# A graph attention kernel: the row carried between superchunks as row 0 of the sums, and 112 nodes per superchunk

## The chip, the cores and the metric

One core of one Trainium2 chip. The time is that of one execution on the device, in microseconds (us). The engines are TensorE (PE, its weight loads PEld), VectorE (DVE), ScalarE (ACT), GpSimd (POOL) and SyncE (SP), each with an instruction stream of its own; they wait for each other through semaphores. In profile lines "L1245" is line 1245 of the kernel file.

## What is computed

Two layers of graph attention over 6250 nodes and 200000 edges (each edge has a source, a destination and 32 attributes; the edges come sorted by destination). Cut to what matters:

```python
def _gat(x, src, dst, ea, Wg, a_s, a_d, Wge, a_e, b, n, h, f):
    hx = (x @ Wg).reshape(n, h, f)
    he = (ea @ Wge).reshape(-1, h, f)
    al = leaky_relu((hx*a_s).sum(-1)[src] + (hx*a_d).sum(-1)[dst] + (he*a_e).sum(-1), 0.2)
    m = segment_max(al, dst)
    al = exp(al - m[dst])
    al = al / segment_sum(al, dst)[dst]
    return segment_sum(hx[src] * al[:, :, None], dst).reshape(n, h * f) + b

def _forward(x, ...):                       # h = 4 heads in layer 0, 1 head in layer 1
    te = relu(edge_attr @ We0 + be0) * exp(x @ Wo0 + bo0)[src][:, None]
    x = relu(_gat(x, *_add_self_loops(src, dst, te, n), ...) + x)     # layer 0
    te = relu(edge_attr @ We1 + be1) * exp(x @ Wo1 + bo1)[src][:, None]
    return _gat(x, *_add_self_loops(src, dst, te, n), ...) + x + orig  # layer 1

h = maximum(layernorm(x), 0)
result = x + _forward(h, ...)
```

## The kernel before

**Tiling.** The sorted edges are cut into 1563 chunks of 128 (one edge per partition), and the chunks into 66 superchunks per layer: 64 of 24 chunks, then one of 14 and one of 13. One superchunk of one layer is a step; there are 132 steps, k = 0 to 131, layer 0 first. A superchunk covers the nodes from its first destination (its base) on; no superchunk of this graph spans more than 102 nodes. Since the edges are sorted, the last node of a superchunk can go on in the next one, so part of its sums must be carried over.

**One step.** For a superchunk, `gather` (POOL, L928) fetches the table row of each edge's source: 24 indirect DMAs of 128 rows into the tile G, with a memset of an unused tile, `gap` (L932), after each. There are three G buffers, and the gathers run two steps ahead: those of step k+2 may start when the sums of step k-1 have read their buffer. `rphase1` makes the edge terms (PE y L1014, ACT R L1019, PE zad L1028), `logits` (DVE, L1115 and on) the attention logits, `links` and `maxima` the running maxima over a node's edges: a PE transpose into lf (L1138), two scans on DVE (L1148, L1150), a transpose back (L1155), then the softmax weights. `scale` (DVE, L1223) multiplies G by the weights, 6.5 us. `onehots` (DVE, L1058) builds S: for each edge of each chunk a one-hot row of 128 columns, by comparing `k_iota` (0 to 127, kept in PSUM) with the edge's destination less the base. `sums` (PE, L1234) adds S^T G over the chunks into u (PSUM, one buffer): row n of u is the sum over the edges of node base + n. `evict` (ACT, L1239) copies u to U.

**The carried row.** `carry` (L1245, L1247) picks the row of the superchunk's last node: PE multiplies `lsel`, a one-hot column with its 1 at the last node's place, with U, and ACT copies the resulting single row to `carry`. In the next step `carried` (DVE, L1208 to L1213) adds that row, times a weight `pr`, to row 0 of the next G before the next `sums`.

**Nodes.** `nodes` loads the 128 table rows from the base on (tw) and, in layer 0, the rows of x. `finish` (merge and nodes, from L1258 on) adds the self loop, divides, and applies the activation, on 128 partitions for a node each. `rows1` to `rows3` make the rows of layer 1's table from it (PE transpose L1329, ACT h1T L1331, PE L424, DVE L428), stored to T[1]; in layer 1 the result goes to out. Neighbouring superchunks overlap in the rows they store; the later store wins. The last two of layer 1 use an indirect store with a bounds check.

**Order.** The order on each engine is written by hand in `edges` (steps up to 60 and 66 to 126 of the main loop), `tight` (near a layer's end) and `last`. In the main loop one step issues, in this order: gathers of the next-but-one superchunk (by `gather(nx)` with its buffer), logits, the edge terms of the next step, links, rows2 of an earlier step, maxima, scale, carried, sums, rows3, onehots of the next step, finish of the previous step, evict, carry, rows1 of the previous step. So on PE, between the sums of one step and the sums of the next, stand in this order: fin of `carry` (waits for U), turned rows L1329, lf L1138, the zad of the node terms (L1073), y L1014, L1155, the table rows L424, the second y, zad, and then the sums, which wait for `carried` and for u to be evicted.

A check on the indices (`chk`) verifies what the fast path assumes, among it that no superchunk spans more nodes than a tile has; otherwise a general path runs.

Of the kernel before, what the change touches and what calls it, by code (L numbers as in the profile page):

```python
# [31 lines left out]
P = 128  # L32
C = 24
SE = P * C
NX = 24
D = 256
ED = 32
PH = 64
BIG = 1e38
PAD_DST = 1 << 20  # L40
END_DST = 1 << 22
EPS = 1e-5
# [36 lines left out]
class Kernel:  # L79
# [31 lines left out]
    def consts(self, wp):  # L111
# [33 lines left out]
                       allow_small_or_imprecise_dtypes=True)  # L145

        self.kps = k = self.ps_k.tile([P, 512], F32, name="kps")
        V.tensor_copy(k[:, 0:P], self.iota_f)
        m32 = wp.tile([P, 1], F32, name="m32", bufs=1)
        self.quad = cp.tile([P, 4], F32, name="quad")  # L150
        nc.gpsimd.memset(self.quad, 0.0)
# [5 lines left out]
        self.k_iota, self.k_part, self.k_w = k[:, 0:P], k[:, P:P + 1], k[:, 2 * P:2 * P + 4 * C + 4]  # L157
        self.wea = []
        for L in self.L:
            wea = cp.tile([P, PH], F32, name=f"wea{L.l}")  # L160
# [269 lines left out]
    def indices(self, wp):  # L430
# [29 lines left out]
        V.tensor_scalar(self.qsel.rearrange("p s k -> p k s"), qd, self.iota_p, None, op0=OP.add)  # L460
        yield

        bcf = wp.tile([NS, 4], F32, name="bcf", bufs=1)
# [32 lines left out]
        V.tensor_scalar(self.base_i[:, 1, :], base[0:1, :], float(N - P), None, op0=OP.min)  # L496
        yield
        ll = wp.tile([P, NS], F32, name="ll", bufs=1)
        V.tensor_sub(ll, last, base)
        self.lsel = cp.tile([P, NS], F32, name="lsel")  # L500
        V.tensor_scalar(self.lsel, ll, self.iota_p, None, op0=OP.is_equal)
        yield
        self.slink = cp.tile([1, NS], F32, name="slink")
        V.tensor_tensor(self.slink, sc0[0:1, 0, :], sc0[0:1, 2, :], op=OP.is_equal)
# [2 lines left out]

        chk = wp.tile([1, 9, NS + 1], F32, name="chk", bufs=1)
        V.memset(chk, 0.0)
        V.tensor_scalar(chk[:, 0, :NS], ll[0:1, :], float(P - 1), None, op0=OP.is_gt)  # L510
# [4 lines left out]
        yield  # L515
        V.memset(nb[:, NS:], float(N))
        V.tensor_sub(nb[:, :NS], nb[:, 1:], nb[:, :NS])
        V.tensor_scalar(chk[:, 1, :NS], nb[:, :NS], float(P), None, op0=OP.is_gt)
        V.tensor_scalar(chk[:, 2, :NS], nb[:, :NS], 0.0, None, op0=OP.is_lt)
        yield  # L520
        V.tensor_tensor(chk[:, 3, :NS], sc0[0:1, 0, :], sc0[0:1, 2, :], op=OP.is_lt)
        if self.direct:
            V.tensor_scalar(chk[:, 4, :self.direct], base[0:1, :self.direct], float(N - P), None, op0=OP.is_gt)
# [87 lines left out]
    def edges(self, ctx):  # L611
# [32 lines left out]
        for k, st in enumerate(steps):  # L644
            nx = steps[k + 1] if k + 1 < len(steps) else None
            for q in steps[k + 1:k + 3]:
                if q["L"] is st["L"] and "tw" not in q:
                    self.nodes(q)
            self.load_lb(k + 2)
            left = self.groups[self.ahead][0] - 2 - k if self.ahead < len(self.groups) else 99  # L650
            if self.rest is None and left <= 2:
                gi = self.index_load(self.ahead, self.xp)
                self.rest = self.index_group(self.ahead, self.xp, gi)
            if st["s"] + 1 == self.NS:
                self.last(st, pv, nx)
# [36 lines left out]
            self.edge_rows(nx)  # L692
            self.onehots(nx)
            if pv:
                drain(self.finish(pv))
            if enter:
                pr = pv
            else:
                self.evict(st)
                self.carry(st)  # L700
                if pv:
                    self.rows1(pv)
                    late = pv
# [23 lines left out]
    def tight(self, st, pv, pr, nx):  # L727
# [36 lines left out]
            self.rows3(pv)  # L764
        drain(self.maxima(st))
        if final:
            self.carry(pv)
            drain(y)
            self.load_ea(st["k"] + 2)
        else:  # L770
            self.evict(pv)
        self.rphase2(nx)
        self.adst(nx)
        if not final:
            self.carry(pv)
            if pr:
                self.rows1(pr)
                self.rows2(pr)
# [10 lines left out]
    def last(self, st, pv, nx):  # L789
# [20 lines left out]
        drain(self.maxima(st))  # L810
        if pv:
            self.evict(pv)
            self.carry(pv)
        drain(self.scale(st, 3))
        self.carried(st)
        self.sums(st)
# [167 lines left out]
    def row(self, i, s):  # L984

        return self.nc.values_load(self.base_i[0:1, i, s:s + 1], engines=(mybir.EngineType.SP,), min_val=0,
                                   max_val=self.N - i * P, skip_runtime_bounds_check_because="destinations are nodes")

    def nodes(self, st):
        nc, L, s = self.nc, st["L"], st["s"]  # L990
        r = self.row(0, s)
        tw = self.np_.tile([P, self.L[0].TW + D], F32, name="tw", bufs=5)
        st["tw"], st["xw"] = tw[:, :L.TW], tw[:, L.TW:L.TW + D]
        w = L.TW + L.l * D
        nc.sync.dma_start(tw[:, :w], self.T[L.l][ds(r, P), 0:w])
        if L.l == 0:
            nc.sync.dma_start(st["xw"], self.a["x"][ds(r, P), :])

    def halves(self, st):

# [30 lines left out]
    def spread(self, st):  # L1031


        if "Q" in st:
            return
        V = self.nc.vector
        q = self.pair(st["k"]) or [st]
        if len(q) < 2 or q[0]["C"] != q[1]["C"]:
            q = [st]
        i, n, s = len(q), 32 * st["C"], st["s"]  # L1040
        lb = st["lb2"] if i > 1 else st["lb"].unsqueeze(1)
        Q = self.wp.tile([P, 2, P], BF, name="Q")
        V.tensor_tensor(lb[:, :, :n], lb[:, :, :n], self.k_part.unsqueeze(2).to_broadcast([P, i, n]), op=OP.is_equal)  # L1043
        V.tensor_tensor(Q[:, :i].rearrange("p i (k j) -> p (i k) j", j=32),
                        self.k_iota[:, 0:32].unsqueeze(1).to_broadcast([P, 4 * i, 32]),
                        self.qsel[:, s:s + i, :].rearrange("p i k -> p (i k)").unsqueeze(2)
                        .to_broadcast([P, 4 * i, 32]), op=OP.is_equal)
# [188 lines left out]
    def evict(self, st):  # L1236
        L = st["L"]
        st["U"] = U = self.np_.tile([P, 272], F32, name="U", bufs=3)
        self.nc.scalar.activation(U[:, :L.W], st["u"][:, :L.W], AF.Copy)  # L1239

    def carry(self, st):
        nc, L, s, U = self.nc, st["L"], st["s"], st["U"]
        if s + 1 < self.NS:
            pr = self.ps_f.tile([P, 512], F32, name="fin")
            nc.tensor.matmul(pr[0:1, :L.W], self.lsel[:, s:s + 1], U[:, :L.W], start=True, stop=True)  # L1245
            st["carry"] = cv = self.wp.tile([1, 272], F32, name="carry")
            nc.scalar.activation(cv[:, :L.W], pr[0:1, :L.W], AF.Copy)  # L1247

    def merge(self, st, wp, w):

# [346 lines left out]
```

## Times and profile before

| what | value |
|---|---|
| median of three runs | 4719.46 us (4714.36 to 4720.51) |
| the profiled execution | 4718.23 us, of which the span of its records 4716.0 us |
| mean granted TensorE clock | 0.732 |
| busy: POOL, PE, DVE, ACT | 3701.8, 3214.2, 2878.5, 574.2 us |
| gathers: number, mean | 3102, 959 ns |
| gap memsets: number, mean | 3102, 221 ns |
| mean period of a steady step, layer 0 and layer 1 | 34.60 us and 34.42 us (start of U to start of U) |

A group line reads: line, engine, operation, output <- inputs, shape, count | busy time, mean ns of one | idle time of the engine just before them, and the releaser that ended most of it. A line of the waits reads: who waited, for whom, total us, times, longest. A timeline line reads: start, duration, engine, line, operation, and in brackets the idle time before it and what ended it. "remote" is a release that the profile can't put down to an instruction of this core. The ends of matmuls are modelled, so the recorded end of a group of matmuls may differ from the moment their result is there.

### The profile page before, as it was taken

What the parts mean: (1) busy time and instruction counts of PE and PEld (TensorE: products, weight loads), DVE (VectorE), ACT (ScalarE), POOL (GpSimd) and SP (SyncE); (2) the same over time, 40 slices, a digit from 0 to 9 for tenths busy, and PEclk for the clock granted to TensorE, in tenths of its full rate; (3) what the DMA queues carried; (4) which work ended last, traced back from release to release, by engine and by line L of the source; (5) the groups of instructions that cost most, each with busy time, mean ns of one, the idle gap of its engine ahead of it and who ended that gap; (6) DMA issues with size and microseconds to landing.
All of it is one profiled execution on the core that took longest, in us unless ns stands there. A gap on an engine that the chain in (4) does not pass through costs nothing.

```text
span 4716.0 us, 38255 instructions
## 1 busy us (share of the span) xinstructions
PE 3214.2 (68%) x10176; PEld 1915.8 (41%) x10176; DVE 2878.5 (61%) x6552; ACT 574.2 (12%) x1282; POOL 3701.8 (78%) x6350
## 2 busy tenths in 40 slices
PE   7777767777677776777655666666666666656666
PEld 6444444444444443444422333434333343433334
DVE  7566767667676676766743555546455555645555
ACT  5111111111111111111100001000000100000010
POOL 5688888888888888888648888888888888888884
PEclk9677777767777777777866677777767776777778
DMA  6344444444444444444323444444444444444442
GB/s 216 111 129 126 136 122 129 134 122 135 127 134 127 124 136 123 132 131 124 107 84 104 128 118 126 125 112 127 120 127 118 126 126 111 127 118 128 118 124 63
DMA packets 236364, 584.09 MB, mean 124 GB/s; under 512 B 63097, under 2 KB 91007, under 8 KB 236073
## 3 DMA queue, kind: packets, MB, share of 16 engines
q0 software_dynamic: 150144, 422.75, 33.8%
q1 hardware_dynamic: 85579, 158.16, 10.1%
q8 instruction: 82, 1.34, 0.1%
q14 instruction: 143, 1.17, 0.1%
q10 hardware_dynamic: 416, 0.67, 0.1%
HBM read 547.11 MB, written 34.33 MB: 123 GB/s over the span
## 4 chain that ended last, share of the span: by engine, by line
DVE 40%; another core or an unknown queue 33%; PE 16%; issue 6%; ACT 4%; POOL 0%; DMA 0%; SPq 0%; DVEq 0%; ACTq 0%; POOLq 0%
DVE G L1223 16%; DVE S L1058 8%; PE y L1014 8%; PE fin L1245 3%; DVE rt L1101 2%; ACT R L1019 1%; ACT U L1239 1%; DVE ade L1104 1%; PE fin L1329 1%; PE u L1234 1%; PE lf L1138 1%; PE zad L1028 1%; DVE mt L1172 1%; DVE m L1175 1%
## 5 line engine op out<-in xcount | busy, mean ns | idle before, releaser
L928 POOL DMA_INDIRECT G<-T,src x3102 | 2974.0, 959 | 938.3 <-issue 498.2
L1234 PE MATMUL u<-G,S 128*128 128x270 f32 (+1 forms) x6252 | 1469.7, 393 | 110.3 <-issue 58.0
L1234 PEld LDWEIGHTS u<-G,S 128*128 128x128 f32 x6252 | 1186.9, 192 | 394.5 <-issue 87.1
L1245 PE MATMUL fin<-U,lsel 128*1 128x270 f32 (+1 forms) x260 | 132.8, 613 | 1143.3 <-ACT U L1239 1136.6
L1223 DVE TENSOR_TENSOR G<-G,kps 128x6144 f32<-128x6144 f32 (+2 forms) x140 | 853.3, 6100 | 0.0
L1014 PE MATMUL y<-ea,webd 64*128 64x384 f32 (+1 forms) x1056 | 754.6, 866 | 89.2 <-issue 65.5
L932 POOL MEMSET gap<- 128x128 f32 x3102 | 684.6, 221 | 4.3 <-remote 1.3
L1148 DVE TENSOR_TENSOR_SCAN cl<-fl,cl,lf 4x129 f32<-4x129 f32 (+1 forms) x130 | 61.2, 471 | 1016.6 <-PE zad L1073 994.3
L1245 PEld LDWEIGHTS fin<-U,lsel 128*1 128x1 f32 x260 | 11.1, 81 | 1202.6 <-ACT U L1239 1201.5
L1028 PE MATMUL zad<-R,wea 128*64 128x384 f32 (+1 forms) x1056 | 474.0, 816 | 0.3 <-DVE aq L1080 0.3
L1014 PEld LDWEIGHTS y<-ea,webd 64*128 64x128 f32 x1056 | 303.3, 317 | 360.3 <-issue 330.0
L1058 DVE TENSOR_TENSOR S<-kps,loc 128x3072 f32<-128x3072 f32 x132 | 436.2, 3305 | 0.0
L1019 ACT ACTIVATE R<-y,webd 128x768 f32<-128x768 f32 x260 | 232.9, 896 | 794.6 <-PE y L1014 348.3
L1028 PEld LDWEIGHTS zad<-R,wea 128*64 128x64 f32 x1056 | 160.4, 207 | 314.9 <-issue 248.5
L1239 ACT ACTIVATE U<-u 128x270 f32<-128x270 f32 (+1 forms) x132 | 51.8, 393 | 1627.1 <-remote 1585.4
L1101 DVE STREAM_TRANSPOSE rt<-zad 128x768 f32<-128x768 f32 (+1 forms) x130 | 125.0, 961 | 27.8 <-remote 15.7
L424 PE MATMUL fin<-wg,h1T 128*128 128x260 f32 x264 | 135.7, 669 | 3.2 <-ACT h1T L1331 3.2
L1043 DVE TENSOR_TENSOR lb<-lb,kps 128x1536 bf16<-128x1536 bf16 (+1 forms) x68 | 113.0, 1662 | 0.0
L424 PE MATMUL ps<-wg,hT 128*128 128x266 f32 x292 | 89.8, 435 | 25.4 <-ACT hT L311 13.9
L424 PEld LDWEIGHTS fin<-wg,h1T 128*128 128x128 f32 x264 | 76.0, 317 | 53.7 <-issue 36.3
L1272 ACT ACTIVATE mw<-mw,mg 128x2 f32<-128x2 f32 x66 | 19.7, 298 | 557.3 <-DVE mw L1264 249.1
L1138 PE MATMUL lf<-ident,fb 128*36 128x128 f32 (+1 forms) x132 | 54.9, 416 | 42.8 <-DVE al L1119 28.2
(193 smaller groups left out, 2269.0 us busy)
## 6 DMA issues: line engine op xcount, KB each, us to landing
G<-T,src POOLq DMA_INDIRECT x3102
ea<-in_ea_dram SPq DMA_DIRECT2D x64, 768.0 KB
lb<-locrow SPq DMA_DIRECT2D x64, 384.0 KB
T<-t1row SPq DMA_DIRECT2D x66, 260.0 KB
tw<-T SPq DMA_DIRECT2D x66, 258.0 KB
tw<-T SPq DMA_DIRECT2D x66, 134.0 KB
tw<-in_x_dram SPq DMA_DIRECT2D x66, 128.0 KB
out_dram<-fb SPq DMA_DIRECT2D x64, 128.0 KB
```

The costliest lines, as they stand in the source:

```text
L424: self.nc.tensor.matmul(ps[:, :L.MW], hT[:, k, :], self.wg[L.l][:, k, :], start=(k == 0), stop=(k == 1))
L928: nc.gpsimd.indirect_dma_start(out=G[:, c, 0:L.TW], out_offset=None, in_=self.rows[L.l][0:n * (1 + L.l), :], in_offset=bass.IndirectOffset ...
L932: nc.gpsimd.memset(self.gap, 0.0)
L1014: nc.tensor.matmul(y[:, o], self.webd[l][r, :], ea[r, w], start=True, stop=True)
L1019: nc.scalar.activation(R[:, i, :32 * c].rearrange("p (b n) -> p b n", b=2), y.rearrange("p (b n) -> p b n", b=2)[:, :, :16 * c], AF.Relu, ...
L1028: nc.tensor.matmul(st["zad"][i * PH:(i + 1) * PH, o], self.wea[l][0], R[:, i, w], start=True, stop=False)
L1043: V.tensor_tensor(lb[:, :, :n], lb[:, :, :n], self.k_part.unsqueeze(2).to_broadcast([P, i, n]), op=OP.is_equal)
L1058: nc.vector.tensor_tensor(st["S"][:, c0:c1, :], self.k_iota.unsqueeze(1).to_broadcast(w), self.loc[:, o + c0:o + c1].unsqueeze(2).to_broad ...
L1101: V.transpose(rv[:, :32 * c].rearrange("p (b n) -> p b n", b=2), z.rearrange("p (b n) -> p b n", b=2)[:, :, :16 * c])
L1223: nc.vector.tensor_tensor(v, v, pw[:, c0:c1, :].unsqueeze(3) .to_broadcast([P, c1 - c0, H, L.F]), op=OP.mult)
L1234: nc.tensor.matmul(st["u"][:, :L.W], S[:, i, :], G[:, i, 0:L.W], start=(j == 0), stop=(j == c - 1))
L1245: nc.tensor.matmul(pr[0:1, :L.W], self.lsel[:, s:s + 1], U[:, :L.W], start=True, stop=True)
```

## The change

The comparison row of the one-hots is shifted by one: column n now stands for node base + n - 1. Columns 1 to 112 are the superchunk's nodes, and column 0 is set, once per step, to the place of the superchunk's last node. So row 0 of the sums is the carried row, in U itself, and `carried` reads it there. `carry` and `lsel` are gone. All that is per node moves up by one partition: tw and x are loaded to partitions 1 to 112, and 112 rows are stored from there. The five tw tiles are made once and set to zero, since rows 0 and 113 to 127 are no longer loaded. The gathers and the memsets between them are as before.

```diff
+M = 112
...
-        V.tensor_copy(k[:, 0:P], self.iota_f)
+        V.tensor_scalar(k[:, 0:P], self.iota_f, -1.0, None, op0=OP.add)
+        V.tensor_copy(k[:, P + 2:P + 34], self.iota_f[:, 0:32])
...
-        ll = wp.tile([P, NS], F32, name="ll", bufs=1)
+        self.lastloc = ll = cp.tile([P, NS], F32, name="lastloc")
         V.tensor_sub(ll, last, base)
-        self.lsel = cp.tile([P, NS], F32, name="lsel")
-        V.tensor_scalar(self.lsel, ll, self.iota_p, None, op0=OP.is_equal)
...
+        self.tws = [self.np_.tile([P, self.L[0].TW + D], F32, name=f"tw{i}", bufs=1) for i in range(5)]
+        for t in self.tws:
+            nc.vector.memset(t, 0.0)
         self.nodes(steps[0])
...
                 self.evict(st)
-                self.carry(st)
...
-        tw = self.np_.tile([P, self.L[0].TW + D], F32, name="tw", bufs=5)
+        tw = self.tws[st["k"] % 5]
...
-        nc.sync.dma_start(tw[:, :w], self.T[L.l][ds(r, P), 0:w])
+        nc.sync.dma_start(tw[1:M + 1, :w], self.T[L.l][ds(r, M), 0:w])
...
-            nc.sync.dma_start(st["xw"], self.a["x"][ds(r, P), :])
+            nc.sync.dma_start(st["xw"][1:M + 1, :], self.a["x"][ds(r, M), :])
...
             st["S"] = self.sp.tile([P, C, P], F32, name="S")
+            nc.vector.tensor_copy(self.k_iota[:, 0:1], self.lastloc[:, st["s"]:st["s"] + 1])
...
-            g, cv = st["G"][0:1, 0, :], st["prev"]["carry"]
+            g, cv = st["G"][0:1, 0, :], st["prev"]["U"]
...
-    def carry(self, st):
-        nc, L, s, U = self.nc, st["L"], st["s"], st["U"]
-        if s + 1 < self.NS:
-            pr = self.ps_f.tile([P, 512], F32, name="fin")
-            nc.tensor.matmul(pr[0:1, :L.W], self.lsel[:, s:s + 1], U[:, :L.W], start=True, stop=True)
-            st["carry"] = cv = self.wp.tile([1, 272], F32, name="carry")
-            nc.scalar.activation(cv[:, :L.W], pr[0:1, :L.W], AF.Copy)
...
-            nc.sync.dma_start(self.T[1][ds(r, P), :], st["trow"])
+            nc.sync.dma_start(self.T[1][ds(r, M), :], st["trow"][1:M + 1, :])
...
-            nc.sync.dma_start(out[ds(r, P), :], o)
+            nc.sync.dma_start(out[ds(r, M), :], o[1:M + 1, :])
         else:
             idx = self.np_.tile([P, 1], I32, name="oidx")
-            nc.vector.tensor_add(idx, self.base_f[:, s:s + 1], self.iota_p)
+            nc.vector.tensor_add(idx, self.base_f[:, s:s + 1], self.iota_m)
+            nc.vector.memset(idx[0:1, :], 1 << 20)
```

Not shown: the second index row with base -1 (`iota_m`), which `qsel` uses too; the limits of the index check, which go from 128 to 112 nodes; and the removal of the other calls of `carry` in `tight` and `last`.

More of the change, by code (lines that the diff above doesn't have):

```diff
@@ L147, in consts @@
         self.kps = k = self.ps_k.tile([P, 512], F32, name="kps")
-        V.tensor_copy(k[:, 0:P], self.iota_f)
+        V.tensor_scalar(k[:, 0:P], self.iota_f, -1.0, None, op0=OP.add)
+        V.tensor_copy(k[:, P + 2:P + 34], self.iota_f[:, 0:32])
+        self.iota_m = cp.tile([P, 1], F32, name="iota_m")
+        nc.gpsimd.iota(self.iota_m, pattern=[[0, 1]], base=-1, channel_multiplier=1,
+                       allow_small_or_imprecise_dtypes=True)
         m32 = wp.tile([P, 1], F32, name="m32", bufs=1)
@@ L156, in consts @@
         V.tensor_add(k[:, P:P + 1], self.iota_p, m32)
-        self.k_iota, self.k_part, self.k_w = k[:, 0:P], k[:, P:P + 1], k[:, 2 * P:2 * P + 4 * C + 4]
+        self.k_iota, self.k_part, self.k_32 = k[:, 0:P], k[:, P:P + 1], k[:, P + 2:P + 34]
+        self.k_w = k[:, 2 * P:2 * P + 4 * C + 4]
         self.wea = []
@@ L459, in indices @@
         self.qsel = cp.tile([P, NS, 4], F32, name="qsel")
-        V.tensor_scalar(self.qsel.rearrange("p s k -> p k s"), qd, self.iota_p, None, op0=OP.add)
+        V.tensor_scalar(self.qsel.rearrange("p s k -> p k s"), qd, self.iota_m, None, op0=OP.add)
         yield
@@ L495, in indices @@
         V.tensor_copy(self.base_i[:, 0, :], base[0:1, :])
-        V.tensor_scalar(self.base_i[:, 1, :], base[0:1, :], float(N - P), None, op0=OP.min)
+        V.tensor_scalar(self.base_i[:, 1, :], base[0:1, :], float(N - M), None, op0=OP.min)
         yield
-        ll = wp.tile([P, NS], F32, name="ll", bufs=1)
+        self.lastloc = ll = cp.tile([P, NS], F32, name="lastloc")
         V.tensor_sub(ll, last, base)
-        self.lsel = cp.tile([P, NS], F32, name="lsel")
-        V.tensor_scalar(self.lsel, ll, self.iota_p, None, op0=OP.is_equal)
         yield
@@ L509, in indices @@
         V.memset(chk, 0.0)
-        V.tensor_scalar(chk[:, 0, :NS], ll[0:1, :], float(P - 1), None, op0=OP.is_gt)
+        V.tensor_scalar(chk[:, 0, :NS], ll[0:1, :], float(M - 1), None, op0=OP.is_gt)
         V.tensor_sub(qd[0:1], qlast[0:1], qbase[0:1])
@@ L517, in indices @@
         V.tensor_sub(nb[:, :NS], nb[:, 1:], nb[:, :NS])
-        V.tensor_scalar(chk[:, 1, :NS], nb[:, :NS], float(P), None, op0=OP.is_gt)
+        V.tensor_scalar(chk[:, 1, :NS], nb[:, :NS], float(M), None, op0=OP.is_gt)
         V.tensor_scalar(chk[:, 2, :NS], nb[:, :NS], 0.0, None, op0=OP.is_lt)
@@ L522, in indices @@
         if self.direct:
-            V.tensor_scalar(chk[:, 4, :self.direct], base[0:1, :self.direct], float(N - P), None, op0=OP.is_gt)
+            V.tensor_scalar(chk[:, 4, :self.direct], base[0:1, :self.direct], float(N - M), None, op0=OP.is_gt)
         V.memset(self.bad[:, 0:1], 0.0)
@@ L766, in tight @@
         if final:
-            self.carry(pv)
             drain(y)
@@ L774, in tight @@
         if not final:
-            self.carry(pv)
             if pr:
@@ L812, in last @@
             self.evict(pv)
-            self.carry(pv)
         drain(self.scale(st, 3))
@@ L986, in row @@
         return self.nc.values_load(self.base_i[0:1, i, s:s + 1], engines=(mybir.EngineType.SP,), min_val=0,
-                                   max_val=self.N - i * P, skip_runtime_bounds_check_because="destinations are nodes")
+                                   max_val=self.N - i * M, skip_runtime_bounds_check_because="destinations are nodes")
     def nodes(self, st):
@@ L1044, in spread @@
         V.tensor_tensor(Q[:, :i].rearrange("p i (k j) -> p (i k) j", j=32),
-                        self.k_iota[:, 0:32].unsqueeze(1).to_broadcast([P, 4 * i, 32]),
+                        self.k_32.unsqueeze(1).to_broadcast([P, 4 * i, 32]),
                         self.qsel[:, s:s + i, :].rearrange("p i k -> p (i k)").unsqueeze(2)
```

## The prediction

> **What bounds the kernel now.** I read the page first (chain, groups), then the waits, then the timeline of a steady step in each layer, then a step where no gather runs.
>
> The page; the chain, and three groups:
> ```profile
> DVE 40%; another core or an unknown queue 33%; PE 16%; issue 6%; ACT 4%; POOL 0%; DMA 0%; SPq 0%; DVEq 0%; ACTq 0%; POOLq 0%
> ...
> L928 POOL DMA_INDIRECT G<-T,src x3102 | 2974.0, 959 | 938.3 <-issue 498.2
> ...
> L1245 PE MATMUL fin<-U,lsel 128*1 128x270 f32 (+1 forms) x260 | 132.8, 613 | 1143.3 <-ACT U L1239 1136.6
> ...
> L1239 ACT ACTIVATE U<-u 128x270 f32<-128x270 f32 (+1 forms) x132 | 51.8, 393 | 1627.1 <-remote 1585.4
> ```
> The instruction pair that the change removes has the largest wait of the page in front of it, but that wait is for U, and U itself waits 1585.4 us for "remote", a releaser that the profile can't name. A third of the chain has no owner. The list of waits says the same by length:
> ```profile
> ACT U L1239 <- remote: 1585.4, 123, 58.5
> ...
> PE fin L1245 <- ACT U L1239: 1136.6, 123, 18.2
> DVE cl L1148 <- PE zad L1073: 994.3, 118, 30.2
> ...
> POOL G L928 <- remote: 285.9, 120, 3.0
> ...
> ACT carry L1247 <- PE fin L1245: 146.1, 128, 2.0
> ```
> The timeline of step 39 (layer 0), one period from U to U being 34.75 us:
> ```profile
> 1515.10 11.27 PE L1234 MATMUL u<-G,S 128*128 128x270 f32 x48 [0.33 <-issue]
> ...
> 1529.02 0.36 DVE L1128 TENSOR_TENSOR_SCAN fb<-pen,al 128x96 f32<-128x96 bf16 x1 [1.14 <-DVE al L1121]
> ...
> 1534.25 0.40 ACT L1239 ACTIVATE U<-u 128x270 f32<-128x270 f32 x1 [9.75 <-remote]
> 1534.49 0.95 POOL L928 DMA_INDIRECT G<-T,src  x1 [2.71 <-remote]
> ...
> 1534.70 1.06 PE L1245 MATMUL fin<-U,lsel 128*1 128x270 f32 x2 [8.34 <-ACT U L1239]
> 1535.79 0.39 ACT L1247 ACTIVATE carry<-fin 1x270 f32<-1x270 f32 x1 [1.15 <-PE fin L1245]
> 1536.23 0.69 PE L1329 MATMUL fin<-ident,fb 128*128 128x128 f32 x2 [0.48 <-ACT carry L1247]
> ...
> 1537.07 2.93 PE L1014 MATMUL y<-ea,webd 64*128 64x384 f32 x4
> ```
> The sums end on record at 1526.37, yet U starts 7.88 us later, and POOL's next gather 0.24 us after U, because its buffer too is released by the sums. The 24 gathers before it run back to back, each 0.95 + 0.17 of issue + 0.22 of gap memset L932 = 1.34 us, from the first one's start at 1499.74 to the last one's end at 1531.55: 31.8 us, then 2.7 us of wait. A step of layer 1:
> ```profile
> 3532.97 10.83 PE L1234 MATMUL u<-G,S 128*128 128x261 f32 x48 [0.17 <-issue]
> ...
> 3554.06 0.39 ACT L1239 ACTIVATE U<-u 128x261 f32<-128x261 f32 x1 [15.62 <-remote]
> 3554.30 0.95 POOL L928 DMA_INDIRECT G<-T,src  x1 [2.15 <-remote]
> ```
> Here the sums end 10.26 us before U. And step 64, where no gather runs:
> ```profile
> 2385.82 2.67 PE L1234 MATMUL u<-G,S 128*128 128x270 f32 x11
> ...
> 2388.53 0.40 ACT L1239 ACTIVATE U<-u 128x270 f32<-128x270 f32 x1 [0.36 <-PE u L1234]
> ```
> U follows the last sum in 0.04 us. So while gathers run, the signal of the sums reaches ACT and POOL late, and what it keeps is its distance to the gathers, not to the sums: over the steady steps U comes 2.46 us (57 steps, layer 0) and 2.26 us (59 steps, layer 1) after the last gather of the group has issued; where sums start 0.5 us later than usual (steps 9, 17, 29, 49, 53), U does not move. The periods are 34.60 and 34.42 us, 0.24 + 31.9 + 2.46 or 2.26. What delays the signal I can't tell from this trace; that it is tied to the gathers is my reading, and the sum hangs on it.
>
> **The change, part by part.**
>
> *Removed: fin<-U,lsel and carry.* Per step two matmuls with their loads and one ACT copy: U to carry's end is 1.93 us (1534.25 to 1536.18), and PE holds turned L1329, lf, the Q zad and y behind it. After the change nothing of PE between the sums and the next sums waits for U. PE can run L1329, lf, zad and y while U is still held; the next sums still need U evicted (one u buffer) and U's row in carried. Today L1155, which the softmax maxima wait for, starts 5.55 us after U (1539.80, behind y). If it may follow U at once, ACT's h1T and R (0.38 + 0.90) still queue behind U, so I count 4.1 us earlier sums in layer 0 (U + 11.5 instead of 15.6). In layer 1 the scan L1148 starts 1.86 us after U (3555.92); about 1.75 go.
>
> What are earlier sums worth? By the tie, little. The nearest row is layer 1 against layer 0: sums 2.35 us earlier after U (13.25 against 15.6), period 0.18 us shorter: 0.077 us per us. Lower bound of the gain 0 (steps 9 to 53: sums 0.5 us apart, U unmoved); upper bound the POOL floor, 24 x 1.34 = 32.2 us, i.e. 2.4 and 2.2 us a step. I take the row: 57 x 4.1 x 0.077 = 18 us and 59 x 1.75 x 0.077 = 8 us, together -26 us (0 to -267, that is 57 x 2.4 + 59 x 2.2).
>
> A rule of the Trainium skill speaks against the tie: SBUF — State Buffer, section "Who interferes with whom", says that a DMA never contends with a compute engine and that TensorE and ScalarE wait on no one. By it the sums' signal would not be late beside gathers, and the waits would be worth their face value; the rows above, 7.9 and 10.3 us beside gathers and 0.04 us without, do not agree, whatever carries the delay.
>
> *Stage ends* (steps 61 to 65, 127 to 131), where U follows PE. In steps 61, 62, 64, 127, 128 and 130 carry ends before or with the scaling L1223 that DVE does anyway (step 62: carry 2335.50, L1223 2336.75): nothing. In steps 63 and 129 fin (1.06 and 1.03 us) stands right ahead of y: -2 us.
>
> *Moved: L1329, lf, zad, y.* They go from after U to before it. TensorE's granted clock is 0.5 from about 2.5 us after the sums until the next sums, so y x4 takes 2.93 us; in step 61, right behind sums, the same y x4 took 1.55 us at clock 1.0. Those 1.4 us lie ahead of U and are in the 4.1.
>
> *Added: the column copy*, one [128x1] DVE op ahead of S: like-sized ops take 0.14 to 0.17 us. In a steady step DVE waits 4.3 us (1532.9 to 1537.17) and 12.0 us (layer 1) for the Q zad, so the 0.17 us is covered; without cover it would be 132 x 0.17 = 22 us. S now also waits for a signal of DVE to itself. Beside late gathers such waits took 1.1 to 1.3 us (L1128 above), early in a group 0.03; S (1516.67) is early. At the stage ends DVE is the bound: 8 x 0.17 = +1.4 us.
>
> *Added: five memsets* of 128x524 on DVE before the first step. L1058's rate, 3305 ns for 3072 columns, gives 0.56 us each, 2.8 us in all; a 128x4 DVE memset took 0.06, 0.3 in all if it goes by count. DVE is partly idle there: 0 to 2.8, I take +1.5.
>
> *112 rows instead of 128.* tw, x, T and out move an eighth less, 268 + 260 KB of traffic a step in layer 0. SP's queue waits for none of it in the steady steps: 0. The extra index memset in the last two out stores: 0.1 us.
>
> Sum against the profiled execution's own 4718.23 (span 4716.0 + 2.2): -26 - 2 + 1.4 + 1.5 + 0.1 = -25, so 4693. The median lies 1.2 above the profiled run: **4694 us**.
>
> **The rivals.**
> 1. *The tie is not strict in layer 1.* There the signal is nearly through when the gathers end: half a sums group (step 127: y behind it ends 4607.83, ACT takes it 4610.52) got through in 9.8 us beside gathers, so a whole one needs some 19.6, and from U + 13.25 that ends at 32.9. Started 1.75 us earlier it ends before the last gather, and U comes up to 2.2 us earlier. Price: layer 1 at the floor, 59 x 2.2 = 130, plus layer 0's 18: 4571; with half of layer 1's, 4636. Against it: layer 0's step 61 held the same y (ended 2283.94, taken 2295.74) until its gathers were over.
> 2. *The waits at face value.* 1.93 x 57 + 1.47 x 59 = 197 us, 4523; POOL's floor in both layers, 267 us, 4452. Against it: step 64's 0.04 us and the unmoved U of steps 9 to 53.
> 3. *Nothing moves.* The tie is strict and the earlier sums only wait longer: -2 + 3 = +1, 4720; with small gains down to 4712.
> 4. *Slower: the hold grows.* L1329, lf, zad and y now run inside the gather group, ahead of U, in step with the late signals. The place is the time from the last gather's issue to U, today 2.46 us in layer 0, which has some 30 more PE, DVE and ACT instructions a step than layer 1 with 2.26. Sixteen to twenty more records ahead of U are at that rate +0.14 us (+16 us over 116 steps); at the 0.40 us that each of the 48 sums takes from start to U (19.05 / 48), two more ahead of U are +0.8 us. I price it at +0.3: +35 us, 4754. It decides as soon as the hold grows by more than the 0.2 us that I count as gain. Against it: PE's order puts them behind the sums.
>
> **How the numbers follow.** Chances: forecast (tie with small gain, own range 4670 to 4712) 0.40; rival 1 0.17; rival 2 0.07; rival 3 0.14; rival 4 0.22. Eight in ten: from 4545, which leaves out rival 2, to 4742, which leaves out the worse half of rival 4. What a measurement here tells from no change is 0.2%, 9 us. Faster by more: 0.37 of the forecast, 0.17, 0.07 = 0.61. Within: 0.03 + 0.14 = 0.17. Slower: 0.22.
>
> **What would show it.** L1245 and L1247 gone; L1329, lf and y starting right behind the sums, before U, with y x4 near 1.55 us; sums at U + 11.5 in both layers; U still 2.2 to 2.5 us behind the last gather of its group; POOL's wait for "remote" near 286 us. If POOL's wait falls to a few us and the period of a layer to 32.2, rival 1 or 2 is right. If U comes 2.7 us or more after the last gather, rival 4. If PE still waits in front of L1329 or lf, the waits moved on instead of going, and the sums don't come earlier.

## The result, and the profile after

The changed kernel is a little slower: 4724.15 us median of 20 runs (4717.92 to 4739.15) against 4716.69 us of the kernel before (4711.08 to 4720.51), ratio 1.0019, 95% interval 1.0013 to 1.0026. The forecast was 4694. The profiled execution took 4732.55 us with a span of 4730.8 us, so it is one of the longer ones.

The page of the changed kernel, chain and groups (line numbers have moved: sums L1238, U L1243, gathers L931, scan L1152):

```profile
POOL 37%; DVE 30%; another core or an unknown queue 14%; issue 10%; PE 6%; DMA 1%; ACT 1%; DVEq 0%; SPq 0%; POOLq 0%; ACTq 0%
...
L931 POOL DMA_INDIRECT G<-T,src x3102 | 2968.3, 957 | 955.1 <-issue 498.6
...
L1152 DVE TENSOR_TENSOR_SCAN cl<-fl,cl,lf 4x129 f32<-4x129 f32 (+1 forms) x130 | 61.3, 471 | 1200.8 <-remote 1090.1
...
L1159 PE MATMUL lf<-ident,cl 36*128 36x36 f32 (+1 forms) x132 | 40.1, 304 | 864.7 <-DVE cl L1154 848.0
...
L1243 ACT ACTIVATE U<-u 128x270 f32<-128x270 f32 (+1 forms) x132 | 51.8, 393 | 2020.3 <-remote 1559.9
```

The matmuls that picked the carried row are gone, and the 1143 us of wait in front of them went nowhere useful. U waits for "remote" about as long as before (1559.9 against 1585.4 us), and another 385 us of its waits now bear the names of zad and y, which U does not read. The scan that follows lf used to wait for a matmul of PE (994.3 us from the node zad) and now waits for "remote" itself (1090.1): lf is computed early, but its signal arrives late as well. PE stands 848 us in front of L1159, one link further on.

A step of layer 0 in the timeline of the changed kernel:

```profile
1514.12 11.21 PE L1238 MATMUL u<-G,S 128*128 128x270 f32 x48 [1.50 <-DVE crow L1215]
...
1528.16 0.33 PE L1142 MATMUL lf<-ident,fb 128*36 128x128 f32 x1 [1.15 <-DVE a L1072]
...
1531.63 1.49 PE L1017 MATMUL y<-ea,webd 64*128 64x384 f32 x2 [0.46 <-issue]
1533.74 0.99 PE L1017 MATMUL y<-ea,webd 64*128 64x384 f32 x1 [0.62 <-issue]
1535.84 0.80 PE L1017 MATMUL y<-ea,webd 64*128 64x384 f32 x1 [1.10 <-issue]
1537.47 0.40 ACT L1243 ACTIVATE U<-u 128x270 f32<-128x270 f32 x1 [13.82 <-PE y L1017]
1537.55 0.47 DVE L1152 TENSOR_TENSOR_SCAN cl<-fl,cl,lf 4x129 f32<-4x129 f32 x1 [7.14 <-PE y L1017]
...
1548.64 11.26 PE L1238 MATMUL u<-G,S 128*128 128x270 f32 x48 [0.36 <-issue]
```

PE does run ahead: lf and y stand between the sums and U. But U and the scan start within 0.08 us of each other, though lf ended 9.06 us before the scan: several signals come through together. y itself is spread over 5.0 us there, with gaps between its matmuls. (The releaser named at U, y, is only the last thing that ended nearby; U reads the sums.) The next sums start 11.17 us after U.

The stages of the two profiled executions, from the starts of U (steps 2, 60, 68 and 126):

| stage | before | after | difference |
|---|---|---|---|
| to U of step 2 | 254.4 | 257.3 | +2.9 |
| layer 0, 58 periods | 2006.7 | 2006.2 | -0.5 |
| change of layer, to step 68 | 329.7 | 329.9 | +0.2 |
| layer 1, 58 periods | 1996.7 | 2012.2 | +15.5 |
| from U of step 126 to the end | 128.5 | 125.2 | -3.3 |

| steady steps | before, layer 0 | after, layer 0 | before, layer 1 | after, layer 1 |
|---|---|---|---|---|
| first sum after U, median | 15.59 | 11.18 | 13.25 | 9.84 |
| U after the end of the last gather, median | 2.46 | 2.41 | 2.28 | 2.42 |
| period, median | 34.59 | 34.56 | 34.40 | 34.39 |
| period, mean | 34.60 | 34.59 | 34.43 | 34.69 |

The sums start 3.4 to 4.4 us earlier and the usual period does not change by 0.05 us. Layer 1's mean is longer than its median because of four pairs of steps: 83 and 84 (33.00 and 39.89 us), 87 and 88 (32.91 and 40.85), 96 and 97 (33.67 and 37.16), 114 and 115 (33.68 and 41.52). Against two usual steps they cost 4.1, 5.0, 2.1 and 6.4 us, 17.6 together. That covers layer 1's loss of 15.5: the kernel before has a long step of its own there (114, 35.83 us). One pair in the timeline, with the usual step ahead of it:

```profile
3074.85 0.39 ACT L1243 ACTIVATE U<-u 128x261 f32<-128x261 f32 x1 [18.86 <-remote]
3074.89 0.47 DVE L1152 TENSOR_TENSOR_SCAN cl<-fl,cl,lf 1x129 f32<-1x129 f32 x1 [13.36 <-remote]
3075.14 0.89 ACT L1022 ACTIVATE R<-y,webd 128x768 f32<-128x768 f32 x1
...
3097.22 1.55 PE L1017 MATMUL y<-ea,webd 64*128 64x384 f32 x4
...
3107.85 0.39 ACT L1243 ACTIVATE U<-u 128x261 f32<-128x261 f32 x1 [17.53 <-remote]
...
3109.24 0.47 DVE L1152 TENSOR_TENSOR_SCAN cl<-fl,cl,lf 1x129 f32<-1x129 f32 x1 [15.39 <-remote]
...
3111.47 0.90 ACT L1022 ACTIVATE R<-y,webd 128x768 f32<-128x768 f32 x1 [3.23 <-PE lf L1159]
```

At 3074.85 U, the scan (which needs lf) and R (which needs y) start within 0.29 us. At 3107.85 U comes 1.4 us early, alone; the gathers restart 0.24 us later, and the scan comes 1.39, R 3.62 us behind U. The next sums start 14.71 us after this U instead of 9.84, and the U after that 7.95 us behind its gathers instead of 2.4. That U follows its sums at once; here it is the sums themselves that are held:

```profile
3122.56 6.10 PE L1238 MATMUL u<-G,S 128*128 128x261 f32 x27
...
3139.49 0.59 PE L1238 MATMUL u<-G,S 128*128 128x261 f32 x1 [1.52 <-issue]
3142.30 5.41 PE L1238 MATMUL u<-G,S 128*128 128x261 f32 x14 [2.21 <-issue]
...
3147.74 0.39 ACT L1243 ACTIVATE U<-u 128x261 f32<-128x261 f32 x1 [7.36 <-PE u L1238]
```

The first 27 matmuls of step 84 run in one go, the next seven start 0.7 to 2.8 us apart beside the gathers, and the last 14 run in one go from 2.5 us behind the last gather. The sums of the long steps 84, 88, 97 and 115 take 20.8 to 26.4 us instead of the usual 10.8. So beside the gathers TensorE is late there not only with its signals but within its own stream; what it stands for there the trace doesn't name ("issue").

### The profile page after: what moved, and what is told of

Read it like the earlier page. It is cut to its first block, busy times and chain, and to the rows that moved or that the text cites. A ratio compares the mean times of both kernels' runs of the same rounds, so it can differ in the third digit from the quotient of the medians.

```text
span 4730.8 us, 37631 instructions
## 1 busy us (share of the span) xinstructions
PE 3051.3 (64%) x9916; PEld 1893.0 (40%) x9916; DVE 2897.0 (61%) x6691; ACT 507.6 (11%) x1152; POOL 3696.2 (78%) x6351
## 4 chain that ended last, share of the span: by engine, by line
POOL 37%; DVE 30%; another core or an unknown queue 14%; issue 10%; PE 6%; DMA 1%; ACT 1%; DVEq 0%; SPq 0%; POOLq 0%; ACTq 0%
POOL G L931 30%; DVE G L1227 8%; POOL gap L935 7%; DVE S L1062 4%; PE u L1238 2%; PE y L1017 2%; DVE lb L1046 1%; DVE rt L1105 1%; DVE a L1072 1%; DMA G<-T,src 1%; DVE a L1074 1%; PE ps L430 1%; DVE G L1119 1%; DVE al L1121 1%
## 5 line engine op out<-in xcount | busy, mean ns | idle before, releaser
L931 POOL DMA_INDIRECT G<-T,src x3102 | 2968.3, 957 | 955.1 <-issue 498.6
L1238 PE MATMUL u<-G,S 128*128 128x270 f32 (+1 forms) x6252 | 1521.8, 402 | 214.3 <-issue 123.9
L1238 PEld LDWEIGHTS u<-G,S 128*128 128x128 f32 x6252 | 1218.9, 197 | 521.4 <-issue 150.0
L1152 DVE TENSOR_TENSOR_SCAN cl<-fl,cl,lf 4x129 f32<-4x129 f32 (+1 forms) x130 | 61.3, 471 | 1200.8 <-remote 1090.1
L1017 PE MATMUL y<-ea,webd 64*128 64x384 f32 (+1 forms) x1056 | 671.0, 773 | 78.4 <-issue 44.2
L1159 PE MATMUL lf<-ident,cl 36*128 36x36 f32 (+1 forms) x132 | 40.1, 304 | 864.7 <-DVE cl L1154 848.0
L1159 PEld LDWEIGHTS lf<-ident,cl 36*128 36x128 f32 (+1 forms) x132 | 23.7, 179 | 969.4 <-DVE cl L1154 949.0
L1017 PEld LDWEIGHTS y<-ea,webd 64*128 64x128 f32 x1056 | 270.5, 282 | 276.6 <-issue 209.0
L1243 ACT ACTIVATE U<-u 128x270 f32<-128x270 f32 (+1 forms) x132 | 51.8, 393 | 2020.3 <-remote 1559.9
L1142 PE MATMUL lf<-ident,fb 128*36 128x128 f32 (+1 forms) x132 | 41.4, 314 | 241.5 <-DVE a L1072 110.0
L1077 PE MATMUL zad<-a,Q 128*128 128x12 bf16 (+1 forms) x132 | 23.9, 181 | 197.2 <-DVE a L1075 176.1
L1142 PEld LDWEIGHTS lf<-ident,fb 128*36 128x36 f32 (+1 forms) x132 | 14.4, 109 | 271.1 <-DVE a L1072 123.1
```

Of the source, the lines that this page charges most:

```text
L931: nc.gpsimd.indirect_dma_start(out=G[:, c, 0:L.TW], out_offset=None, in_=self.rows[L.l][0:n * (1 + L.l), :], in_offset=bass.IndirectOffset ...
L1017: nc.tensor.matmul(y[:, o], self.webd[l][r, :], ea[r, w], start=True, stop=True)
L1159: nc.tensor.transpose(pc, cl[:n, 0:P], self.ident[0:n, 0:n])
L1238: nc.tensor.matmul(st["u"][:, :L.W], S[:, i, :], G[:, i, 0:L.W], start=(j == 0), stop=(j == c - 1))
```

## The experiments

The experiments ran on six chips, one after another, each with the kernel before beside it. On chip 10 the kernel before took 4718 us, as in the result, on four others 4377 to 4384 us, and on the last 4756. That turned out to matter more than any edit: where it takes 4718 or 4756, signals are late beside gathers ("late chips": numbers 10 and 1), where it takes some 4380 they are not (7, 12, 3 and 11). No chip came up twice, so what belongs to the chip and what to the occasion can't be told apart.

**TensorE waits for U again.**

```diff
                 self.evict(st)
+                self.hold_pe(st)
...
+    def hold_pe(self, st):
+        U = st["U"]
+        pr = self.ps_f.tile([P, 512], F32, name="fin")
+        self.nc.tensor.matmul(pr[0:1, 0:2], U[:, 0:1], U[:, 0:2], start=True, stop=True)
```

> The changed kernel, with one matmul of one row and two columns that reads U put where the carry stood in the main loop's order, so that TensorE waits for U again before L1325, lf, the node zad and y (its result is not used). Theory A, left-over signals: TensorE's signals get through slowly beside gathers, what is left gets through in POOL's pause between two groups; in the changed kernel U sometimes gets through ahead of lf and y behind it, gathers restart, and the next step is 3 to 7 us late (layer 1: steps 84, 88, 97, 115). With nothing issued ahead of U there is nothing left over: no step of layer 1 above 36 us except one where SP is late, its mean period 34.4, and the time 4 to 8 us under the changed kernel's: 4717 to 4721, within 0.1% of the kernel before. Rival B, added work: the loss is the memsets and the column copies on VectorE; then it stays at 1.0019 of before.

On chip 10: 4722.15 us (11 runs, 4717.98 to 4725.49), 1.0009 of before (1.0000 to 1.0018), 1 us above the range expected. The trace has no pair: the longest steps of layer 1 are 35.98 us (step 114, which is 35.83 in the kernel before) and otherwise within 0.5 us of 34.5. Layer 1 takes 1997.8 us, against 2012.2 in the changed kernel; the start is 2.7 us late, as there. Its sums start at U + 14.30 and 12.41 and the usual periods are 34.53 and 34.39, again unmoved. So without the run ahead of U the pairs are gone, as theory A's first half says. This rests on one trace of each kernel; the times fit it, as these 11 runs spread over 7.5 us and the changed kernel's 20 over 21. The step at the same place, in its timeline:

```profile
3109.89 0.39 ACT L1244 ACTIVATE U<-u 128x261 f32<-128x261 f32 x1 [16.26 <-remote]
...
3110.34 0.19 PE L1249 MATMUL fin<-U 128*1 128x2 f32 x2 [11.52 <-ACT U L1244]
...
3110.81 2.93 PE L1018 MATMUL y<-ea,webd 64*128 64x384 f32 x4
3110.91 0.47 DVE L1153 TENSOR_TENSOR_SCAN cl<-fl,cl,lf 1x129 f32<-1x129 f32 x1 [13.76 <-PE zad L1078]
```

Here everything behind U is computed after U, and the scan follows it in 1.02 us.

**POOL waits for the scan.**

```diff
-            self.gather(nx)
             drain(self.logits(st))
...
             self.links(st)
+            nc.gpsimd.tensor_copy(self.gap[0:1, 0:1], st["cl"][0:1, P:P + 1])
+            self.gather(nx)
```

> The changed kernel, with the gathers of the next group issued only after the scans of links (a one-element copy on POOL reads the scan's result), so POOL's pause lasts until lf has come through; TensorE still runs ahead of U. Theory A: no pair of a short and a long step is left in layer 1; each steady step is longer by the time from U to the end of the scans plus the copy, 0.6 to 1.2 us, so period 35.1 to 35.7 in both layers and the time 4715 + 116 x 0.6 to 1.2, 4785 to 4855. Rival B: as many long steps in layer 1 as in the changed kernel, on top of that.

5226.21 us, 1.1079 of before: far outside, and no test. The logits in front of that scan wait for the gathers' landing (1746.5 us in its list of waits, "DVE G L1120 <- DMA G<-T,src"), so the edit made a loop of gathers, logits, lf, scan and the next gathers: `gather(nx)` is that of the next superchunk, not of the next but one as the order above has it, and it now waited for a scan that needs the gathers just ahead of it. I had not followed what the scan itself waits for.

**Half the gathers.**

```diff
         for c in (range(c0, last + 1) if c0 else (last, *range(last))):
+            if st["k"] > 3 and last == C - 1 and c % 2 == 0:
+                continue
```

> The changed kernel, gathering only every second chunk of the full superchunks from step 4 on (12 gathers instead of 24; the other chunks keep old rows, so the output is not the reference's). Theory A, the hold is tied to the gathers: the group lasts 16 us and is over before the sums end, U follows the last sum at once (0.04 us), period 21 to 24 us, time 3200 to 3500. Rival C, the time from the first sum to U (23.4 us) belongs to TensorE itself, whatever POOL does: period 33 to 35, time 4600 to 4700.

3446.65 us, periods of 26.37 and 23.13 us (medians; the first is above what I expected). Chip 10 still, in the timeline:

```profile
999.88 0.96 POOL L937 DMA_INDIRECT G<-T,src  x1 [0.17 <-issue]
...
1001.94 11.21 PE L1244 MATMUL u<-G,S 128*128 128x270 f32 x48 [0.32 <-DVE G L1223]
1013.18 0.40 ACT L1249 ACTIVATE U<-u 128x270 f32<-128x270 f32 x1 [1.73 <-PE u L1244]
```

With the last gather issued before the sums, U starts 0.03 us after the recorded end of the last one. U is at once behind its sums in all steady steps. The hold belongs to the gathers, on the same chip and with the same sums. Rival C is out.

**No memsets between the gathers.** The line `nc.gpsimd.memset(self.gap, 0.0)` and its condition are left out, in the changed kernel.

> The changed kernel without the memsets between the gathers. Theory A1, the group's length alone sets the period: 24 x 1.12 = 26.9 us plus 2.7 of pause, period 29.6 in both layers and the time near 4150. Theory A2, the memsets are the time in which signals get through: then without them less gets through, the hold grows, and the period does not fall below 34 us, or rises.

4800.66 us on chip 10, 1.0182 of before (1.0166 to 1.0197). The group is 30.0 us instead of 31.9, but U comes 5.45 (layer 0) and 4.15 us (layer 1) behind it, and the periods are 35.74 and 34.24. Theory A2 is nearer, but only layer 0 got longer. There the hold sits in the sums, as in the pairs: they take 21.4 us at the median instead of 11.2, and in 47 of 58 steps U follows their last matmul within 0.1 us.

**A chip without the hold.** The changed kernel again, on chip 7, and with one more memset in the middle of each full group of layer 1, with and without the wait for U; and the kernel before with the five fixed, zeroed tiles.

```diff
             if st["k"]:
                 nc.gpsimd.memset(self.gap, 0.0)
+            if L.l == 1 and last == C - 1 and c == 11:
+                nc.gpsimd.memset(self.gap, 0.0)
```

> The changed kernel again, for a second trace. Theory A: it has 2 to 6 pairs again in layer 1, a step under 34.0 us followed by one over 36, each pair 2 to 7 us longer than two usual steps, and each starting in one of the steps in which POOL stops 0.45 instead of 0.17 us between two gathers (in the first trace steps 69, 74, 78, 83, 87, 91, 96, 100, 105, 109, 114, 118, 122; pairs began at 83, 87, 96 and 114). Its single times spread over 15 us or more. If pairs begin elsewhere, that stop is not what starts them.

> The changed kernel with one more gap memset in the middle of each group of layer 1, i.e. a stop of POOL of 0.22 + 0.17 us in every one of its 64 full steps instead of in every fourth or fifth. Theory A: the pairs become frequent, 15 or more of them at 2 to 7 us, on top of at most 64 x 0.39 = 25 us for the memsets: +60 to +200 us against the changed kernel. Rival D, the long steps are chance and have nothing to do with POOL's stops: at most +25 us.

> The same extra memset in layer 1, in the kernel in which TensorE waits for U ahead of L1325, lf, zad and y. Theory A: nothing lies behind U that could be left over, so no pairs, and at most +25 us against that kernel without the extra memset (4722); less, if the stop lets signals of the sums through that would otherwise need the pause at the end. Rival D: the same as in the run without the wait.

> The kernel before with five fixed tw tiles that are set to zero by VectorE before the first step, as in the changed kernel, and nothing else. If the 3.0 us by which the changed kernel's first steps are later are those memsets (2.71 us in its trace), this is 3 us over the kernel before: 4720 to 4722, its first U near 187.9 us instead of 184.9, and the steady periods as before.

There the kernel before took 4377.07 us. The changed kernel: 4371.73, 0.9984 (0.9975 to 0.9993), a little faster. The page of the changed kernel there:

```profile
POOL 79%; issue 12%; PE 4%; DVE 4%; DMA 0%; ACT 0%; POOLq 0%; DVEq 0%; ACTq 0%; SPq 0%
...
L931 POOL DMA_INDIRECT G<-T,src x3102 | 2972.4, 958 | 610.1 <-issue 521.5
...
L1243 ACT ACTIVATE U<-u 128x270 f32<-128x270 f32 (+1 forms) x132 | 51.8, 393 | 496.6 <-PE u L1238 496.6
```

"Remote" is gone from U, which starts 0.04 us after the last sum in the midst of gathers; POOL runs from group to group and is the bound, with mean periods of 31.98 and 32.27 us, the floor of 32.2 that the prediction worked out. Single steps of layer 1 alternate between some 30 and some 34.5 us, but none takes over 35.4: there are no pairs as theory A means them, and without late signals the run is no test of it. (The list of steps in the expectation has 114 among those with a stop of 0.45 us. In the first trace that stop is in 127 and not in 114.) The extra memset cost 4392.24 - 4371.73 = 20.5 us, and 4391.53 with the wait for U, the same: where POOL is the bound each of the 64 memsets costs 0.32 us, and whether TensorE runs ahead makes no difference. The zeroed tiles: 4380.64, 1.0007 (0.9998 to 1.0016), +3.6 us, which noise alone could give; by the medians the rest of the change is worth 4371.73 - 4380.64 = -8.9 us there. The trace of that kernel has 2982.3 us of gathers where the changed one has 2972.4, 3 ns less for each of 3102; that is as large as the gain, but what shortens them (an eighth less traffic beside them, or the missing work) was not tried.

**Chip 12.** The same again, with the tiles set to zero one by one ahead of their first load, in the kernel that waits for U:

```diff
-        for t in self.tws:
-            nc.vector.memset(t, 0.0)
...
         tw = self.tws[st["k"] % 5]
+        if st["k"] < 5:
+            nc.vector.memset(tw, 0.0)
```

> The changed kernel a third time. The second time the kernel before took 4377 us beside it, not 4717, and no signal was late there (U 0.04 us after the last sum). If the kernel before takes some 4717 us in this call, signals are late here: theory A then expects 1.0005 to 1.003 of before, 2 to 6 pairs in layer 1, each starting in a step with a stop of POOL of 0.45 us inside the group. If it takes some 4377, the changed kernel is at 0.998 to 0.999 again and has no hold.

> The changed kernel with one more gap memset in the middle of each full group of layer 1, again. Where signals are late (before at some 4717): theory A, 15 or more pairs, +60 to +200 us against the changed kernel; rival D (the long steps have nothing to do with POOL's stops), at most +25 us. Where they are not late (before at some 4377): 64 x 0.39 = 25 us at most, as POOL is the bound there.

> The same extra memset in the kernel in which TensorE waits for U ahead of L1325, lf, zad and y. Where signals are late: theory A, no pairs and at most +25 us against 4722; rival D, as much as in the run without the wait. Where they are not late: +20 us.

> The kernel in which TensorE waits for U, with the five tw tiles set to zero one by one, each ahead of its first load, instead of all five ahead of the first step. The first load then waits for one memset instead of five: 2.2 us less than 4722 where signals are late, within 0.1% of the kernel before.

The kernel before took 4380.66 us, the changed kernel 4372.64, 0.9982 (0.9973 to 0.9991); with the extra memset 1.0035 (1.0022 to 1.0048), with it and the wait for U 1.0028 (1.0018 to 1.0038); w_early 4372.49, 0.9981 (0.9972 to 0.9990), no different from the changed kernel. It was not run on a late chip, which its expectation was about.

**Chip 3.** The changed kernel with and without the extra memset, and the kernel before without the memsets between its gathers.

> The changed kernel with one more gap memset in the middle of each full group of layer 1, a third time. Where signals are late (before at some 4717): theory A, 15 or more pairs of a short and a long step in layer 1, +60 to +200 us against the changed kernel; rival D (the long steps have nothing to do with POOL's stops), at most +25 us. Where they are not late (before at some 4377): +20 us, as twice before.

> The changed kernel, beside the run above. Where signals are late: 1.0005 to 1.003 of before, 2 to 6 pairs in layer 1, each starting in a step with a stop of POOL of 0.45 us inside its group. Where they are not: 0.998.

> The kernel before without the memsets between the gathers. Where signals are late: theory A2 as in the changed kernel without them, slower by 50 to 100 us, 4770 to 4820. Where they are not late, POOL sets the period: 24 x 0.39 = 9.4 us less of POOL time a step if gathers keep their 0.95 us, so the period falls to what TensorE and VectorE need, 24 to 28 us, and the time to 3600 to 3900; if it stays above 4300, the memsets only fill time in which the next gather could not have started anyway.

The changed kernel is at 0.9984 again (0.9974 to 0.9993), with the extra memset at 1.0034 (1.0022 to 1.0045). Without memsets the kernel before takes 4098.61 us, 0.9351 (0.9336 to 0.9367). The page of that kernel, its chain and its gathers:

```profile
DVE 35%; POOL 31%; PE 13%; issue 12%; DMA 6%; ACT 2%; DVEq 0%; SPq 0%; ACTq 0%; POOLq 0%
...
L928 POOL DMA_INDIRECT G<-T,src x3102 | 2950.4, 951 | 1036.2 <-issue 918.5
```

The gathers keep their 0.95 us, but some six tenths of the 686 us that the memsets took come back as issue time between gathers (918.5 us against 498.2 in the trace of before). So the mean period falls to 29.8 and 30.1 us, not to the 24 to 28 that I gave, and the time lies between the two outcomes that I had set.

**Chips 11 and 1.** The extra memset and the missing memsets once more.

> The changed kernel with one more gap memset in the middle of each full group of layer 1, once more, for a chip on which signals are late. There (before at some 4717): theory A, 15 or more pairs of a short and a long step in layer 1, 4785 to 4925; rival D, at most 4750. Where they are not late (before at some 4380): 4395 to 4400.

> The changed kernel without the memsets between the gathers, which took 4800.66 us where the kernel before took 4717.79. Where signals are late, the same again, 1.018 of before. Where they are not: the kernel before without the memsets took 0.9351 of before, and the change itself 0.998, so 0.930 to 0.936, 4075 to 4100 us, which would be the fastest version there.

> The changed kernel with one more gap memset in the middle of each full group of layer 1, a last time, for a chip on which signals are late. There (before at some 4717): theory A, 15 or more pairs of a short and a long step in layer 1, 4785 to 4925; rival D, at most 4750. Where they are not late (before at some 4380): 4395 to 4400, and the question stays open.

Chip 11: the changed kernel without memsets 4115.00, 0.9385 (0.9370 to 0.9401), just outside the 0.930 to 0.936 expected; with the extra memset 4398.90 (one run), as the three times before. So against the kernel before, the changed kernel without memsets is 1.8% slower on chip 10 and 6% faster on chip 11, and the kernel before without them 6.5% faster on chip 3. That last one is the fastest version measured that does all the work, where signals are not late.

Chip 1, the last, was a late one (before 4756.04, with the extra memset 4760.29, one run each). Its trace has two pairs, steps 83 and 84 (30.34 and 44.60 us) and 87 and 88 (33.18 and 41.20), and no other, although every full group of layer 1 had the extra memset. Theory A had asked for 15 or more: its second half, that any stop of POOL inside a group starts a pair, is wrong. The added stop is not quite the one of the first trace, though: it is a memset, always in the middle of the group, where that one is idle time at a place that changes from group to group. What remains is that two of the pairs begin in the same steps, 83 and 87, in the result and on chip 1. In the trace of the result three of the four begin in one of the 13 steps in which POOL stands 0.44 or 0.45 us instead of 0.17 between two gathers (83, 87, 96); step 114 has instead a first gather that starts 1.71 us after the U before it. What comes with that stop and lets U through early stays open.

## Why the prediction was wrong

**Where it failed.** The term "-26 us" for earlier sums. The prediction read the tie in the main rightly, U held until a group of gathers is over, and then still priced earlier sums at 0.077 us per us, from layer 1 against layer 0. That row compares two layers that differ in much else. The sums came 4.4 us earlier in layer 0 (4.1 was the forecast) and 3.4 in layer 1 (1.75), and the usual periods moved by 0.03 and 0.01 us; in the kernel with the wait for U, with sums 1.3 and 0.8 us earlier than before, by 0.06 and 0.01. So on the late chip the term measured nothing in the usual steps. The lower bound that stood beside it, 0 from the steps with late sums, was the right value: it came from the same layer, from steps that differ in the start of the sums. With it the sum is rival 3, at most 4720 us, and that is what the usual steps did. Nor is U's distance to the last gather, which the prediction took as what U keeps, quite fixed. In the 12 steady steps of layer 1 of the changed kernel's trace in which POOL makes a stop of 0.45 us, the group is 0.30 us longer and U comes 0.29 us sooner behind it (31.99 + 2.16 against 31.69 + 2.45 us): the period stays, as if a stop inside the group counted like the pause at its end.

**What was missing.** Rival 4 had the side right, and its place in part: work that PE issues ahead of U delays what comes after. But that is not its mechanism. In the usual steps the period did not grow: U came 2.41 us behind the gathers in layer 0 (2.46 before) and 2.42 in layer 1 (2.28), where the group was 0.15 us shorter. The price is paid in a few pairs, where U gets through without what PE had issued behind it and the next sums are held half way. That the change came out slower, as rival 4 had it, is in part luck: it priced +35 us, spread over all steps. In the profiled execution the pairs are 17.6 us, and the trace with the wait for U has none. That the changed kernel's 20 runs spread over 21 us and those of before over 9 fits a number of pairs that differs from run to run; only profiled executions show them, so this is argued, not shown. At the median, 4724.15 - 4716.69 = +7.5 us, there is room for 2.9 of memsets, -3.3 at the end and some 8 of pairs.

**The other steps.** The memsets were sized at +1.5 between 0 and 2.8; they took 2.71 us in one piece ahead of the first load, nothing hid them, and the first steps are 2.9 us late. The column copy takes 0.15 us and S starts 0.04 us after it, hidden as forecast. The stage ends, -2 + 1.4, came to +0.2 and -3.3. Fewer rows moved were priced at nothing, and on a late chip nothing shows. That y x4 takes 1.55 us right behind the sums came true in layer 1; in layer 0 it is spread over 5.0 us in front of U, with gaps of its own.

**What was seen as certain and is not.** The hold itself. It is there on two of six chips. The Trainium skill, SBUF — State Buffer, section "Who interferes with whom", says that a DMA never contends with a compute engine. That section is about the ports into SBUF and says nothing of signals, so the prediction drew more from it than it states. In the traces, four chips show no delay (0.04 us from the last sum to U beside gathers) and two do (7 to 14 us). No trace of one chip could have told that. On the three of the other four where the change alone was run, it is 0.16 to 0.18% faster, 5 to 8 us, still far from the -26 us.

## What to carry to other kernels

When a wait is tied to another engine's work, moving its own producer earlier may be worth nothing, as here, and a slope taken between two stages that differ in several ways is no price; use steps of one stage that differ in one thing. An instruction that waits can keep the ones behind it out of a queue that is not flowing: before removing such a wait, ask what will now be standing in the queue when it opens. Tune pauses between transfers on more than one chip: without the same memsets, the changed kernel is 1.8% slower than the kernel before on one and 6% faster on another.

## What the runs showed of the hardware that was not expected

The same program took 4377 to 4384 us on four chips and 4717 to 4756 us on two. On the two, while POOL issues indirect gathers, signals of TensorE reach other engines 7 to 14 us late, and mostly all at once when the gathers end; in some steps TensorE's own matmuls stand too, up to 2.8 us from one start to the next. With half the gathers, on the same chip, the signal takes 0.03 us. It is not an effect of being profiled: 4718.23 us profiled, 4719.46 not, for the kernel before. What differs between the chips, or between the occasions on which they ran, the traces don't tell.
